# Turning 64x64 adjacency matrices on VectorE instead of TensorE in a four-layer graph network

## The chip, the cores and the metric

The kernel runs on one core of one Trainium2 chip. The metric is the device time of one execution in microseconds (us), taken as the median of several runs; smaller is better. Before the change it is 2506.93 us, the median of three runs between 2506.72 and 2507.49. The profile that this document reads is of one execution with a span of 2505.0 us from its first to its last instruction.

A core has five engines with a queue each. TensorE (PE in the profile, with PEld for its weight loads) multiplies matrices and can turn a 128x128 tile by multiplying with the identity. VectorE (DVE), ScalarE (ACT) and GpSimd (POOL) do elementwise work. SyncE (SP) issues transfers. Each engine takes its own instructions in the order of the program; between engines they wait on semaphores.

## What is computed

The input is 128 graphs of 64 nodes with 256 features each, with one 64x64 adjacency matrix of zeros and ones for each graph. Four layers follow one another, each adding to x what it makes of the normalized x. Cut to what matters:

```python
# layer 0: attention with 8 heads, masked by the adjacency
scores = where(adj > 0, q @ k.T / sqrt(32), -9e15);      x += softmax(scores) @ v @ Wo + bo
# layer 1: attention, biased by the logarithm of the adjacency
scores = q @ k.T / sqrt(32) + log(adj + 1e-6);           x += softmax(scores) @ v @ Wo.T + bo
# layer 2: five rounds of a gated graph network
for l in range(5):
    agg = A.T @ (h @ weight[l])                          # A = (adj != 0)
    h = gru_cell(agg, h)
x += h * mask
# layer 3: gated graph convolution
norm  = (sum(abs(adj), -1) + 1e-6) ** -0.5
f_hom = adj @ (x @ theta * norm) * norm
x += elu(gate * f_hom + (1 - gate) * f_het)
```

Everything is in 32-bit floats.

## The kernel before

Two graphs make a pair and fill 128 partitions; four pairs (512 tokens) make a group, and there are 16 groups. The adjacency of two groups is loaded at once as `adjq`, with the 128 rows of a pair on the partitions and 64 columns for each of 8 pairs in the free dimension.

The adjacency is needed in three forms. The attention works on scores that lie with the keys on the partitions, and multiplies exp(scores) by a mask: for layer 0 `(adj > 0) * 2^32` and for layer 1 `(adj + 1e-6) * 2^32`. Both masks need the adjacency turned. Layer 2 takes it as it lies (`A`). Layer 3 multiplies by its transpose, as a 128x128 matrix for each pair with the two 64x64 blocks on the diagonal, scaled by `norm` (`adjT`).

The kernel is built twice into the program, first in this fast form (`lean`) and then in a careful form that runs only if a test on the data asks for it; on these inputs it does not run.

The masks, at the start of a group's part in the first two layers:

```python
masks = [new(f"mask{layer}", [P, PAIRS, NODES], 2, ...) for layer in range(2)]
ps_m = bank(f"mask_{g}")                                 # one of four PSUM banks
def turn_adj():
    for half in range(2):
        p = first + 2 * half
        nc.tensor.transpose(ps_m[:, half * P : (half + 1) * P],
                            adjq[:, p : p + 2, :].rearrange("p t k -> p (t k)"), ident.tile)
pe(220, turn_adj, [adjq, ident], [ps_m], holds=masks, mode=TURN)
for layer, (by, op) in enumerate(((0.0, ALU.is_gt), (1e-6, ALU.add))):
    vec(dve(256), lambda ...: nc.vector.tensor_scalar(
        masks[layer]..., ps_m[:, : 2 * P], by, MASK_UP, op0=op, op1=ALU.mult), [ps_m], [masks[layer]])
```

And the matrix for layer 3, at the end of that part. `blk` is one tile for the whole kernel, filled with zeros once:

```python
for gp in range(2):
    s = slice(gp * NODES, (gp + 1) * NODES)
    pool(350, lambda s=s: nc.gpsimd.tensor_copy(blk[s, :, s], adjq[s, sel, :]), [adjq], [(blk, gp)])
A = ...                                                  # one VectorE instruction on adjq
...                                                      # deg and norm
ps = bank(f"adjT_{g}")
def turn():
    for p in range(PAIRS):
        nc.tensor.transpose(ps[:, p * P : (p + 1) * P], blk[:, p, :], ident.tile)
pe(437, turn, [blk, ident], [ps], holds=[adjT], mode=TURN)
for p in range(PAIRS):
    sca(act(P, 1), lambda p=p: nc.scalar.activation(
        adjT[:, p, :], ps[:, p * P : (p + 1) * P], AF.Identity, scale=norm[:, p : p + 1]), ...)
```

None of these calls is emitted where it stands. `pe`, `vec`, `vec2`, `sca` and `pool` record an operation with a cost from fixed formulas of the author, and a planner (`Plan.run`) puts all operations of the kernel into the order of each engine. It plays a list scheduling through with those costs, and takes at each step the operation with the lowest key that can start:

```python
def dve(n, ptr=0):                                       # assumed ns of a VectorE operation
    return n * 1.042 + 68 + 60 * ptr
WIDE, T64, T32, TURN = range(4)                          # how TensorE's array is divided
CHANGE = ((0, 95, 95, 0), (250, 30, 135, 200), (237, 135, 30, 187), (0, 95, 95, 0))
BESIDE = 0.45                                            # how much small products are drawn together
...
if mode in (T64, T32):
    return -BESIDE if last in (T64, T32) else ALONE if small < 2 else 0.0
```

So a change of any operation can move every other one. Most products are on the whole 128x128 array (WIDE). Three are on a divided array: the aggregation of layer 2 (`agg`, 64x64, 80 times), the scores (`s`, 64x64, 64 times), and the weighing of the values by the attention (`o`, 32 columns wide, 64 times). `CHANGE` holds what the author takes a change between these to cost.

While one group is in layer 2, the next is in layers 0 and 1 and the one before is in layer 3; the planner interleaves the three.

## Time and profile before

| what | measured |
|---|---|
| time | 2506.93 us |
| TensorE busy | 2483.1 of 2505.0 us |
| VectorE busy | 1875.7 us in 4396 instructions |
| ScalarE busy | 1304.8 us |
| GpSimd busy | 889.4 us |
| turning for the masks | 32 TensorE matmuls |
| turning for layer 3 | 64 TensorE matmuls, after 32 GpSimd copies |
| masks out of PSUM | 32 VectorE instructions, 402 ns each on average |

In the profile a row names a line of the kernel, an engine, an operation, and the tile written and the tiles read; then comes how often it occurs, its busy time in all in us, and the mean duration of one in ns. A product in 32-bit floats shows as two matmul records, since the array takes it in two passes; a transpose shows as one. Matmuls follow one another closer than their durations, because they are pipelined: for what one costs, the distance from its start to the next start is read, and for that the timeline, which lists the instructions of one engine in order of time, with equal neighbours merged. The same holds, less strongly, for VectorE.

### The profile page before, as it was taken

What the parts mean: (1) busy time and instruction counts of PE and PEld (TensorE: products, weight loads), DVE (VectorE), ACT (ScalarE), POOL (GpSimd) and SP (SyncE); (2) the same over time, 40 slices, a digit from 0 to 9 for tenths busy, and PEclk for the clock granted to TensorE, in tenths of its full rate; (3) what the DMA queues carried; (4) which work ended last, traced back from release to release, by engine and by line L of the source; (5) the groups of instructions that cost most, each with busy time, mean ns of one, the idle gap of its engine ahead of it and who ended that gap; (6) DMA issues with size and microseconds to landing.
All of it is one profiled execution on the core that took longest, in us unless ns stands there. A gap on an engine that the chain in (4) does not pass through costs nothing.

```text
span 2505.0 us, 58714 instructions
## 1 busy us (share of the span) xinstructions
PE 2483.1 (99%) x24057; PEld 2131.6 (85%) x24057; DVE 1875.7 (75%) x4396; ACT 1304.8 (52%) x2654; POOL 889.4 (36%) x894
## 2 busy tenths in 40 slices
PE   9999999999999999999999999999999999999997
PEld 7888888888888888888888888888888888888885
DVE  6666777777777777787778777777777777877667
ACT  3455454555555455555554555555554555555544
POOL 6633433333333332423334333333333424333221
PEclk9999999999999999999999999999999999999999
DMA  6411212112222121222113122122221212211120
GB/s 207 171 61 64 94 62 88 65 53 84 72 80 72 62 74 65 82 69 80 59 62 102 50 88 83 52 81 72 80 68 59 76 66 80 72 46 71 49 71 19
DMA packets 78266, 188.60 MB, mean 75 GB/s; under 512 B 14802, under 2 KB 66852, under 8 KB 67108
## 3 DMA queue, kind: packets, MB, share of 16 engines
q1 hardware_dynamic: 77872, 184.71, 21.6%
q8 instruction: 192, 3.15, 0.5%
q14 instruction: 86, 0.70, 0.1%
q10 hardware_dynamic: 116, 0.04, 0.0%
HBM read 166.70 MB, written 18.02 MB: 74 GB/s over the span
## 4 chain that ended last, share of the span: by engine, by line
PE 97%; DVE 2%; ACT 0%; issue 0%; POOL 0%; DMA 0%; DVEq 0%; ACTq 0%; POOLq 0%
PE gb L994 22%; PE gc L994 17%; PE nb L994 11%; PE nc L994 8%; PE qkvb L711 6%; PE qkvc L711 5%; PE y L879 4%; PE agg L1034 3%; PE l3b L1339 3%; PE s L775 2%; PE l3c L1339 2%; PE lnT L547 2%; PE hT L547 2%; PE o L843 2%; PE o L851 1%; PE gv L930 1%
## 5 line engine op out<-in xcount | busy, mean ns | idle before, releaser
L1103 POOL TENSOR_TENSOR sn<-h,sn 128x512 f32<-128x512 f32 x158 | 205.5, 1304 | 664.3 <-ACT sn L1101 664.3
L994 PE MATMUL gb<-Ta,gv 128*128 128x256 f32 x960 | 248.1, 381 | 0.0
L994 PE MATMUL gb<-Th,w_hh 128*128 128x256 f32 x960 | 247.9, 381 | 0.0
L963 POOL TENSOR_TENSOR Th<-h 128x256 f32<-128x256 f32 x160 | 120.4, 772 | 333.6 <-PE nb L994 230.6
L533 POOL TENSOR_TENSOR rstd<-pw,few 128x2 f32<-128x2 f32 x128 | 94.9, 741 | 382.6 <-DVE pw L532 380.6
L799 POOL TENSOR_TENSOR e<-e,mask 128x512 f32<-128x512 f32 x128 | 176.2, 1396 | 105.9 <-ACT e L797 105.9
L994 PEld LDWEIGHTS gb<-Th,w_hh 128*128 128x128 f32 x960 | 177.5, 190 | 23.4 <-issue 1.9
L994 PEld LDWEIGHTS gb<-Ta,gv 128*128 128x128 f32 x960 | 177.1, 191 | 23.4 <-issue 2.1
L1101 ACT ACTIVATE sn<-sn,b_n 128x512 f32<-128x512 f32 x158 | 113.4, 722 | 132.9 <-DVE sn L1099 132.5
L994 PE MATMUL gc<-h,w_hh 128*128 128x256 f32 x640 | 167.4, 384 | 0.1
L994 PE MATMUL gc<-agg,gv 128*128 128x256 f32 x640 | 164.6, 380 | 0.0
L1105 DVE SCALAR_TENSOR_TENSOR sn<-sg,sn 128x512 f32<-128x512 f32 x158 | 107.4, 686 | 62.9 <-POOL sn L1103 62.6
L1086 ACT ACTIVATE sg<-sg,b_rz 128x512 f32<-128x512 f32 x158 | 106.6, 715 | 90.3 <-DVE sg L1066 90.2
L963 POOL TENSOR_TENSOR Th<-h,Th 128x256 f32<-128x256 f32 x160 | 144.8, 905 | 8.6 <-DVE h L1107 2.9
L1097 DVE SCALAR_TENSOR_TENSOR sn<-sg,sn 128x512 f32<-128x512 f32 x158 | 118.6, 758 | 37.1 <-ACT sn L1208 30.5
L994 PE MATMUL nb<-Th,w_hh 128*128 128x256 f32 x480 | 144.5, 383 | 0.1
L994 PE MATMUL nb<-Ta,gv 128*128 128x256 f32 x480 | 144.3, 382 | 0.0
L994 PEld LDWEIGHTS gc<-h,w_hh 128*128 128x128 f32 x640 | 117.0, 190 | 23.4 <-issue 2.5
L879 PE MATMUL y<-w_L_gnn_Wo,oT 128*128 128x256 f32 x512 | 135.6, 380 | 0.1
L994 PEld LDWEIGHTS gc<-agg,gv 128*128 128x128 f32 x640 | 120.7, 190 | 16.0 <-issue 0.2
L1047 DVE TENSOR_TENSOR Ta<-agg 128x256 f32<-128x256 f32 x160 | 88.7, 574 | 50.8 <-PE nb L994 33.0
L1107 DVE SCALAR_TENSOR_TENSOR h<-sn 128x512 f32<-128x512 f32 x158 | 122.2, 780 | 5.6 <-ACT e L797 0.5
(228 smaller groups left out, 6527.2 us busy)
## 6 DMA issues: line engine op xcount, KB each, us to landing
gv<-gates SPq DMA_DIRECT2D x80, 1344.0 KB, 5.9
qw<-kept SPq DMA_DIRECT2D x203, 192.0 KB, 2.5
x<-in_x_dram SPq DMA_DIRECT2D x32, 256.0 KB, 3.4
out_dram<-x SPq DMA_DIRECT2D x32, 256.0 KB, 2.9
gates<-gv SPq DMA_DIRECT2D x5, 1344.0 KB, 4.9
adjq<-in_adj_dram SPq DMA_DIRECT2D x8, 256.0 KB, 5.2
gw<-in_L_gnn_weight_dram SPq DMA_DIRECT2D x5, 256.0 KB, 6.4
kept<-s SPq DMA_DIRECT2D x8, 128.0 KB, 3.4
```

The lines of the kernel that those rows point to most:

```text
L711: nc.tensor.matmul(bk[:, j * P : (j + 1) * P], lhs, rhs, start=first and j == 0, stop=True, skip_group_check=True)
L799: pool(1000, lambda e=e: nc.gpsimd.tensor_tensor(e.tile, e.tile, bias_at(pp)[:, None, :].to_broadcast([P, 4, 2 * NODES]), op=ALU.mult), [e ...
L879: pe(mm(256), lambda i=i, c=c: nc.tensor.matmul(py[:, i * D : (i + 1) * D], oT[:, i, c, :], w_o[:, c, :], start=c == 0, stop=c == 1), [(oT ...
L963: pool(690, lambda: nc.gpsimd.tensor_tensor(T[:, i, :], x(), y(), op=ALU.subtract), reads, [(T, i)])
L994: nc.tensor.matmul(bank_[:, col * HALF : (col + 1) * HALF], at(g, n), rhs(), start=first and j == 0, stop=True, skip_group_check=True)
L1086: sca(act(TOK, 1.5), lambda k=k, col=col: nc.scalar.activation(g_v[:, :, k, :], g_v[:, :, k, :], AF.Tanh, bias=b_rz[:, col : col + 1], sca ...
L1097: vec2(dve(TOK), lambda: nc.vector.scalar_tensor_tensor(a_(), r(), 1.0, a_(), op0=ALU.add, op1=ALU.mult), [*ts[0], n_v], [n_v])
L1101: sca(act(TOK, 1.5), lambda: nc.scalar.activation(a_(), a_(), AF.Tanh, bias=b_n[:, oc : oc + 1]), [n_v, b_n], [n_v])
L1103: pool(1230, lambda: nc.gpsimd.tensor_tensor(b_(), hh(), a_(), op=ALU.subtract), [*hp, n_v], [n_v])
L1105: vec2(dve(TOK), lambda: nc.vector.scalar_tensor_tensor(b_(), z(), 1.0, b_(), op0=ALU.add, op1=ALU.mult), [*ts[1], n_v], [n_v])
L1107: vec2(dve(TOK), lambda: nc.vector.scalar_tensor_tensor(hh(), b_(), 0.5, a_(), op0=ALU.mult, op1=ALU.add), [n_v], hp)
L1339: pe(mm(384), lambda: nc.tensor.matmul(bk[:, : 3 * P], b(), w3[:, :, n, :], start=first, stop=True, skip_group_check=True), [w3, *reads], ...
```

## The change

The turning moves from TensorE to VectorE. VectorE's transpose instruction turns each 32x32 block in place. A 64x64 matrix consists of four such blocks, and a pair of graphs of eight; when the instruction's output starts at another group of 32 partitions than its input, the block is also moved, and with all blocks moved the whole matrix is turned. So neither the identity nor PSUM is needed.

For the masks, 16 instructions for each group take 32 partitions and two pairs' blocks each (32x64 elements), from every one of the four groups of 32 partitions to every one. They write into the tile of layer 1's mask; both masks are then made from that tile, in SBUF, the second in place. For layer 3, 8 instructions (32 partitions, four pairs, 32x128 elements) put the turned blocks directly into `blk`, which takes the place of the two GpSimd copies, the four TensorE transposes and the PSUM bank; ScalarE then scales out of `blk`.

```diff
         if lean:
             masks = [...]
-            ps_m = bank(f"mask_{g}")
-            def turn_adj(): ...            # two nc.tensor.transpose
-            pe(220, turn_adj, [adjq, ident], [ps_m], holds=masks, mode=TURN)
+            adj_part = lambda: adjq[:, sel, :].rearrange("q (half t) k -> q half t k", t=2)
+            turned_adj = lambda: masks[1].tile.rearrange("q (half a) n -> q half (a n)", a=2)
+            for block in range(16):
+                frm, to = block // 4, block % 4
+                vec(dve(64), lambda frm=frm, to=to: nc.vector.transpose(
+                    turned_adj()[to * 32 : (to + 1) * 32, :, frm * 32 : (frm + 1) * 32],
+                    adj_part()[frm * 32 : (frm + 1) * 32, :, to // 2, to % 2 * 32 : (to % 2 + 1) * 32]),
+                    [adjq], [(masks[1], block)])
             for layer, (by, op) in enumerate(((0.0, ALU.is_gt), (1e-6, ALU.add))):
                 vec(dve(256), lambda ...: nc.vector.tensor_scalar(
-                    masks[layer]..., ps_m[:, : 2 * P], by, MASK_UP,
-                    op0=op, op1=ALU.mult), [ps_m], [masks[layer]])
+                    masks[layer].tile, masks[1].tile, by, MASK_UP, op0=op, op1=ALU.mult),
+                    [masks[1]], [masks[layer]])
...
         for gp in range(2):
             s = slice(gp * NODES, (gp + 1) * NODES)
-            pool(350, lambda s=s: nc.gpsimd.tensor_copy(blk[s, :, s], adjq[s, sel, :]), [adjq], [(blk, gp)])
+            if not lean: ...               # as before
+            for block in range(4):
+                frm, to = (slice(lo, lo + 32) for lo in (gp * NODES + block // 2 * 32, gp * NODES + block % 2 * 32))
+                col = slice(block % 2 * 32, (block % 2 + 1) * 32)
+                vec(dve(128), lambda frm=frm, to=to, col=col: nc.vector.transpose(
+                    blk[to, :, frm], adjq[frm, sel, col]), [adjq], [(blk, (gp, block))])
...
-        ps = bank(f"adjT_{g}")
+        ps = blk if lean else bank(f"adjT_{g}")
+        turned_blk = (lambda p: blk[:, p, :]) if lean else (lambda p: ps[:, p * P : (p + 1) * P])
-        pe(437, turn, [blk, ident], [ps], holds=[adjT], mode=TURN)
+        if not lean:
+            pe(437, turn, [blk, ident], [ps], holds=[adjT], mode=TURN)
         for p in range(PAIRS):
             sca(act(P, 1), lambda p=p: nc.scalar.activation(
-                adjT[:, p, :], ps[:, p * P : (p + 1) * P], AF.Identity, scale=norm[:, p : p + 1]),
+                adjT[:, p, :], turned_blk(p), AF.Identity, scale=norm[:, p : p + 1]),
                 [ps, norm], [(adjT, p)])
```

None of the planner's own numbers is changed.

## The prediction

> **What bounds the kernel now.** First the busy times of the page, then its chain that ended last:

> ```profile
> PE 2483.1 (99%) x24057; PEld 2131.6 (85%) x24057; DVE 1875.7 (75%) x4396; ACT 1304.8 (52%) x2654; POOL 889.4 (36%) x894
> ...
> PE 97%; DVE 2%; ACT 0%; issue 0%; POOL 0%; DMA 0%; DVEq 0%; ACTq 0%; POOLq 0%
> ```

> TensorE is busy 99% of the span and makes up 97% of the chain. A table of windows says where the rest lies: from 400 to 2300 us TensorE is busy in 1899.5 of 1900 us; of the 22 us it idles, 17 lie after 2300 us, where the last group has no neighbour to fill in, and most of the others at the start. So there is no wait inside to remove: time is what TensorE's instructions take, one after the other, plus a start and a tail. VectorE, at 75%, has idle time, but it feeds TensorE.

> The rows that the change removes, from the groups of TensorE and GpSimd by shape:

> ```profile
> L1280 PE MATMUL adjT<-ident,adjblk 128*128 128x128 f32 x64 | 9.7, 275 | 0.0
> L1231 PE MATMUL mask<-ident,adjq 128*128 128x128 f32 x32 | 6.2, 274 | 0.0
> L1265 POOL COPY adjblk<-adjq 64x256 f32<-64x256 f32 x32 | 13.1, 411 | 37.4 <-PE adjT L1280 36.4
> ```

> The 275 ns are a duration in a pipeline, not a cost. From the starts in the trace, two transposes in a row are 109 ns apart (median of 981 pairs), and a 128x256 pass 216 ns from the next. GpSimd waits before its copies, but it is idle 64% of the time and bounds nothing.

> The timeline of TensorE shows a second cost, that of dividing the array (start, duration, instruction, count):

> ```profile
> 1166.50 0.38 PE L1231 MATMUL mask<-ident,adjq 128*128 128x128 f32 x2
> 1166.81 0.45 PE L843 MATMUL o<-e,v 64*32 64x64 f32 x32
> ...
> 1214.95 0.59 PE L994 MATMUL nb<-Ta,gv 128*128 128x256 f32 x2
> 1215.48 1.16 PE L1034 MATMUL agg<-A,ht 64*64 64x64 f32 x64
> 1216.57 1.13 PE L994 MATMUL gb<-h,w_hh 128*128 128x256 f32 x4
> ...
> 1185.45 1.03 PE L994 MATMUL gb<-h,w_hh 128*128 128x256 f32 x4
> 1186.41 1.16 PE L1034 MATMUL agg<-A,ht 64*64 64x64 f32 x64
> 1187.39 1.06 PE L775 MATMUL s<-kexp,qk 64*64 64x128 f32 x32
> 1188.38 0.92 PE L994 MATMUL gb<-Ta,gv 128*128 128x256 f32 x3
> ```

> An aggregation alone takes 1216.57 - 1214.95 less two passes of 0.216, that is 1.19 us. Scores alone, read in the same way at 359 us, take 1.13. An aggregation with scores directly behind takes 1188.38 - 1185.45 less four passes: 2.07 instead of 2.32. So a neighbour on the same kind of array saves **0.25 us**. By the same reading a weighing alone takes 1.38 us, and beside an aggregation or scores the pair takes 0.09 less. Before the weighing above stands a transpose, and the array is divided at the same price: the last transpose start to the first `o` start is 203 ns in the trace, 94 more than 109, as it is 309 instead of 216 behind a full product. Taking the transpose away neither saves nor costs a change.

> [...] 294 ns (row L1423, 128x256 out of SBUF) against 402 ns for the masks out of PSUM.

> **The change, part by part.**

> *Removed from TensorE*: 16 groups x (2 + 4) transposes = 96, at 109 ns: **-10.5 us**, all on the path.

> *Moved on TensorE*: the order of the changed program is fixed when it is built, so I counted it. Full-array products and the other transposes are as many as before. The divided ones are not placed as before:

> | what stands together | before | changed |
> |---|---|---|
> | aggregation and scores | 26 | 3 |
> | weighing and scores | 29 | 30 |
> | aggregation and weighing | 14 | 2 |
> | alone (agg, s, o) | 40, 9, 21 | 75, 31, 32 |

> The planner, its weights tuned to the old operations, has lost 23 pairs worth 0.25 us and 11 worth 0.09: 5.8 + 1.0 = **+6.8 us**, on the path. What is left of the gain is 3.7 us.

> *Added to VectorE*: these rows carry the estimate, from the groups of VectorE by shape:

> ```profile
> L863 DVE STREAM_TRANSPOSE zt<-rz 128x256 f32<-128x256 f32 x128 | 50.0, 416 | 0.0
> L732 DVE TENSOR_TENSOR v<-qkvb,q 128x128 f32<-128x128 f32 x58 | 16.4, 282 | 0.0
> L1268 DVE TENSOR_SCALAR A<-adjq 128x256 f32<-128x256 f32 x16 | 15.4, 960 | 11.3 <-PE agg L1034 11.3
> L1236 DVE TENSOR_SCALAR mask<-mask 128x256 f32<-128x256 f32 x32 | 12.5, 402 | 1.7 <-PE mask L1231 1.7
> ```

> A transpose of 256 columns takes 416 ns and an operation of 128 columns 282, so about 1.05 ns a column on 148 ns. Estimate: 148 + 64 x 1.05 = 215 ns for a mask block, 282 for a block of layer 3. If each is held, that is its cost: 256 x 0.215 + 128 x 0.282 = 55 + 36 = 91 us. The 32 mask operations should gain some 0.1 us each, 3.5 us, unless they are slowed as row L1268 is: the same sort of operation, whose 16 instances range from 279 to 1374 ns, the fastest near the 294 of L1423. In the ten slow ones a subtraction on GpSimd (row L1103) had begun 54 to 62 ns earlier, and they end about 150 ns after it: an operation of this sort waits while GpSimd's runs. The planner reckons with this for L1268, but not for the masks, which read PSUM until now. VectorE's busy time becomes about 1963 us, 78% of the span: beside TensorE's work, no bound by its sum.

> *Its bursts*: the planner assumes 64 x 1.042 + 68 = 135 ns for a mask block and 201 for the others. Held, they take 80 ns more each: 1.3 us for the 16 masks of a group, 0.65 us for the 8. In the changed order of a middle group 13 mask blocks stand before and between the subtractions `Ta` of the fifth round, and 5 blocks of layer 3 around those of the first. What follows stands late by these amounts. How much room is there? By TensorE's order, between the end of the aggregation and the first product that reads `Ta` stand 18 us of other products in the fifth round, but only 5.9 in the first; two copies by ScalarE (0.6 each) and the first subtraction (0.42) have to fit in there with their signals, and with the blocks about 1.5 us more. That fits. VectorE's order also holds things with less room, so I allow 0 to 0.4 us of stall a group, **+2 us** with a middle of 0.13 x 16.

> *Removed from GpSimd and PSUM*: 13 us of copies and two of the uses of the four PSUM banks for each group. GpSimd is not the bound, and TensorE has hardly a stall that a free bank could end: 0.

> *The start*: TensorE's first mask turn came at 9.34 us, between projections. Now 16 blocks (about 3.5 us) stand on VectorE before the columns of biases and the first `qk`, which began at 10.44 and 10.70. They come some 1.5 us late; the changed order puts products for the fused weights ahead of the first scores. Within 1 us either way: 0.

> Sum: 2506.9 - 10.5 + 6.8 + 2 = **2505 us**.

> **Rivals.** *Removal counts in full*: if the lost pairs cost less than I read, or the old schedule paid for them elsewhere, 2497 us. Against it: the 0.25 and the 0.09 come from starts in the trace, and the counts from the program. *VectorE's lateness becomes the wait*: if each group stalls TensorE by 1 us, through held blocks and slowed masks, 2519 us. For it speaks that VectorE is in the inner loop (its row `sg` already waits for TensorE's `gc`, and TensorE in turn for it now and then) and that the planner's costs are too low by 2 us a group; against it, that in the before kernel row L1268 overruns its assumed 250 ns by 1.1 us in most groups, and TensorE still runs without a gap. *VectorE as the bound*: 78% is far from it. *A hidden change*, with nothing to measure: 2507, quite possible, for two terms of opposite sign nearly cancel.

> **Range and chances.** The removal is sure to 0.5 us, the pairs to 1.5, the stalls run from 0 to 12, start and tail to 3 either way. So the range is 2497 to 2514. Two per cent are 50 us: TensorE would have to shed five times what is removed, or to stall 3 us in every group. Faster 0.01, within 2% 0.97, slower 0.02.

> **What would show it right or wrong.** TensorE: 96 records fewer, 23961; busy about 2480; no rows for `mask` and `adjT`; aggregation and scores mostly apart in the timeline, still 1.19 and 1.13 us each. VectorE: 384 instructions more, 4780; new transposes near 215 and 282 ns with the next start not before the end; busy near 1963. The mask row: near 294 ns on average if undisturbed, up to 1370 where GpSimd works. If a transpose across quadrants takes 400 ns or more, the bursts double and the stalls with them. If TensorE idles by more than 10 us between 400 and 2300 us, the second rival holds; the waits then name a row of VectorE. If TensorE's busy time falls to 2473, I was wrong on the pairs.

## The result, and the profile after

The changed kernel takes **2575.38 us** (median of four runs, 2573.0 to 2576.19) against 2507.21 for the kernel before beside it: a ratio of **1.027, with an interval of 1.0252 to 1.0288**. It is slower by 68 us. The prediction was 2505 us, and its range ended at 2514.

The page of the changed kernel, first the busy times, then the chain that ended last:

```profile
PE 2509.7 (98%) x23961; PEld 2132.1 (83%) x23961; DVE 1962.5 (76%) x4780; ACT 1306.0 (51%) x2654; POOL 865.3 (34%) x862
...
PE 79%; DVE 15%; ACT 3%; issue 2%; POOL 0%; DMA 0%; DVEq 0%; ACTq 0%
```

TensorE has its 96 records fewer, and yet is busy 27 us longer. VectorE's share of the chain rose from 2% to 15%. The span is 2572.9 us, of which TensorE now idles 63 instead of 22. So two questions: what is TensorE waiting for, and why does less work take it longer?

The list of waits answers the first (us in all, times, longest). First the row of the kernel before, then of the changed one:

```profile
PE gc L994 <- DVE sg L1066: 0.6, 2, 0.4
```

```profile
PE gc L994 <- DVE sg L1066: 28.2, 24, 2.1
```

`gc` is a PSUM bank with gate sums of layer 2, and `sg` is VectorE's addition that reads it. The next products into the bank wait until it is read, up to 2.1 us by the row above:

```python
vec(dve(512), lambda: nc.vector.tensor_tensor(dst_at(), src(), other.tile, op=ALU.add), [bk, other], writes)   # sg, L1066
```

The timeline shows one such place, first TensorE (start, duration, instruction, count, idle time before it and its releaser):

```profile
925.58 0.59 PE L879 MATMUL y<-w_L_gnn_Wo,oT 128*128 128x256 f32 x2
926.01 0.60 PE L547 MATMUL lnT<-ident,xn 128*128 128x128 f32 x4
928.72 2.05 PE L994 MATMUL gc<-Th,w_hh 128*128 128x256 f32 x4 [2.11 <-DVE sg L1066]
930.56 1.76 PE L994 MATMUL gc<-Ta,gv 128*128 128x256 f32 x4
932.16 0.60 PE L994 MATMUL nc<-Th,w_hh 128*128 128x256 f32 x2
```

and VectorE in the same stretch:

```profile
921.47 2.22 DVE L1230 STREAM_TRANSPOSE mask<-adjq 32x64 f32<-32x64 f32 x9
923.72 0.43 DVE L1047 TENSOR_TENSOR Ta<-agg 128x256 f32<-128x256 f32 x1
924.18 0.98 DVE L1230 STREAM_TRANSPOSE mask<-adjq 32x64 f32<-32x64 f32 x4
...
926.30 0.74 DVE L1230 STREAM_TRANSPOSE mask<-adjq 32x64 f32<-32x64 f32 x3
927.08 0.69 DVE L1097 SCALAR_TENSOR_TENSOR sn<-sg,sn 128x512 f32<-128x512 f32 x1
927.69 0.29 DVE L1235 TENSOR_SCALAR mask<-mask 128x256 f32<-128x256 f32 x1
927.89 0.68 DVE L1066 TENSOR_TENSOR sg<-gc,p1g 128x512 f32<-128x512 f32 x1
```

VectorE has no gap: 16 mask blocks, four `Ta`, one `sn`, one mask, and only then `sg`, which ends at 928.57. TensorE's last product before it ends at 926.61, and it goes on at 928.72. From the last use of `gc` (the four passes just before 925.15) to its next stand only two passes for `nc`, two for `y` and one turn `lnT` of four transposes: 1.3 us of work, and VectorE is late by more. In this way 11 of the groups each lose 2.27 us, the distance from the last transpose to the next pass, 2.38, less the usual 0.109.

The second question is answered by what follows the wait. The four passes at 928.72 take until 930.56, 1.84 us; in the kernel before four take 4 x 0.216 = 0.86. The table of windows shows why (window, us, busy time and count of PE, PEld, DVE, ACT, POOL, then TensorE's clock, the share of DMA and its GB/s):

```profile
921.00:926.00 5.00, 5.00 (x24) 4.34 (x24) 4.74 (x18) 1.52 (x3) 3.85 (x6) 1.00 0.65 230
926.00:929.00 3.00, 0.89 (x6) 0.67 (x5) 2.93 (x8) 0.60 (x1) 0.00 (x0) 0.94 0.21 81
929.00:932.50 3.50, 3.50 (x10) 2.83 (x10) 3.50 (x11) 0.86 (x2) 1.27 (x1) 0.56 0.00 0
932.50:936.00 3.50, 3.50 (x21) 3.17 (x20) 2.03 (x7) 2.03 (x5) 1.71 (x2) 1.00 0.01 2
```

After the idle time of 2.11 us the granted clock is 0.5 for 3.41 us (the trace's record of the clock; the window's 0.56 is its mean over 3.5 us), and 10 instructions stand where the next window has 21. This costs another 1.7 us, half of the 3.41. It happened after 9 of the 11 waits and once at the start, after an idle time of 3.0 us: 10 x 1.7 = 17 us. This is most of why TensorE's busy time grew with less to do: in experiment 3, which has none of these drops, it is 2492.4 us.

The new instructions, from the tile views of the changed kernel (count: duration in ns, least, median and most, first and last start in us):

```profile
L1230 DVE STREAM_TRANSPOSE mask<-adjq x256: 199/236/242, 8.2 to 2025.5; 32x64 f32<-32x64 f32 x128
...
L1235 DVE TENSOR_SCALAR mask<-mask x32: 281/294/984, 12.5 to 2030.1; 128x256 f32<-128x256 f32 x32
```

```profile
L1270 DVE STREAM_TRANSPOSE adjblk<-adjq x128: 265/302/309, 45.8 to 2070.2; 32x128 f32<-32x128 f32 x128
```

From one mask block's start to the next are 250 ns (median of 211 pairs with nothing between), against 236 ns of duration; for layer 3 it is 315 against 302. So each starts 13 to 14 ns after the end of the one before (this is what "held" means here and in the recorded texts), while the `Ta` at 925.19 and 925.53 above start 0.34 us apart and last 0.43. The planner, which assumed 135 and 201, is 115 ns short for each.

### The profile page after: what moved, and what is told of

Read it like the earlier page. It is cut to its first block, busy times and chain, and to the rows that moved or that the text cites. A ratio compares the mean times of both kernels' runs of the same rounds, so it can differ in the third digit from the quotient of the medians.

```text
span 2572.9 us, 58794 instructions
## 1 busy us (share of the span) xinstructions
PE 2509.7 (98%) x23961; PEld 2132.1 (83%) x23961; DVE 1962.5 (76%) x4780; ACT 1306.0 (51%) x2654; POOL 865.3 (34%) x862
## 4 chain that ended last, share of the span: by engine, by line
PE 79%; DVE 15%; ACT 3%; issue 2%; POOL 0%; DMA 0%; DVEq 0%; ACTq 0%
PE gb L994 19%; PE gc L994 14%; PE nb L994 9%; PE nc L994 6%; PE qkvb L711 5%; PE qkvc L711 4%; PE y L879 3%; PE agg L1034 3%; PE l3b L1347 2%; DVE mask L1230 2%; DVE Ta L1047 2%; PE o L843 2%; PE s L775 2%; PE l3c L1347 2%; PE hT L547 2%
## 5 line engine op out<-in xcount | busy, mean ns | idle before, releaser
L1103 POOL TENSOR_TENSOR sn<-h,sn 128x512 f32<-128x512 f32 x158 | 205.0, 1301 | 802.7 <-ACT sn L1101 802.7
L994 PE MATMUL gb<-Th,w_hh 128*128 128x256 f32 x960 | 250.9, 384 | 0.0
L994 PE MATMUL gb<-Ta,gv 128*128 128x256 f32 x960 | 246.5, 379 | 0.0
L799 POOL TENSOR_TENSOR e<-e,mask 128x512 f32<-128x512 f32 x128 | 182.9, 1449 | 69.5 <-ACT e L797 68.6
L994 PEld LDWEIGHTS gb<-Th,w_hh 128*128 128x128 f32 x960 | 177.9, 192 | 30.4 <-DVE sg L1066 4.0
L994 PEld LDWEIGHTS gb<-Ta,gv 128*128 128x128 f32 x960 | 179.3, 190 | 23.1
L1105 DVE SCALAR_TENSOR_TENSOR sn<-sg,sn 128x512 f32<-128x512 f32 x158 | 122.2, 774 | 76.1 <-POOL sn L1103 75.8
L994 PE MATMUL gc<-h,w_hh 128*128 128x256 f32 x640 | 166.1, 382 | 0.1
L994 PE MATMUL gc<-agg,gv 128*128 128x256 f32 x640 | 164.3, 379 | 0.0
L994 PE MATMUL nb<-Ta,gv 128*128 128x256 f32 x480 | 144.4, 382 | 0.0
L994 PE MATMUL nb<-Th,w_hh 128*128 128x256 f32 x480 | 143.1, 380 | 0.0
L963 POOL TENSOR_TENSOR Th<-h,Th 128x256 f32<-128x256 f32 x160 | 133.4, 834 | 9.3 <-DVE h L1107 2.7
L1107 DVE SCALAR_TENSOR_TENSOR h<-sn 128x512 f32<-128x512 f32 x158 | 131.7, 840 | 5.7 <-DVE sn L1105 0.5
L994 PEld LDWEIGHTS gc<-h,w_hh 128*128 128x128 f32 x640 | 117.7, 190 | 21.4 <-ACT sg L1093 0.5
L1097 DVE SCALAR_TENSOR_TENSOR sn<-sg,sn 128x512 f32<-128x512 f32 x158 | 118.2, 756 | 20.1 <-ACT sn L1208 12.5
L1093 ACT ACTIVATE sg<-sg,b_rz 128x256 f32<-128x256 f32 x158 | 71.6, 500 | 121.8 <-DVE sg L1066 119.8
L994 PEld LDWEIGHTS gc<-agg,gv 128*128 128x128 f32 x640 | 118.6, 190 | 17.3
```

What stands on the lines that cost most here:

```text
L799: pool(1000, lambda e=e: nc.gpsimd.tensor_tensor(e.tile, e.tile, bias_at(pp)[:, None, :].to_broadcast([P, 4, 2 * NODES]), op=ALU.mult), [e ...
L963: pool(690, lambda: nc.gpsimd.tensor_tensor(T[:, i, :], x(), y(), op=ALU.subtract), reads, [(T, i)])
L994: nc.tensor.matmul(bank_[:, col * HALF : (col + 1) * HALF], at(g, n), rhs(), start=first and j == 0, stop=True, skip_group_check=True)
L1097: vec2(dve(TOK), lambda: nc.vector.scalar_tensor_tensor(a_(), r(), 1.0, a_(), op0=ALU.add, op1=ALU.mult), [*ts[0], n_v], [n_v])
L1103: pool(1230, lambda: nc.gpsimd.tensor_tensor(b_(), hh(), a_(), op=ALU.subtract), [*hp, n_v], [n_v])
L1105: vec2(dve(TOK), lambda: nc.vector.scalar_tensor_tensor(b_(), z(), 1.0, b_(), op0=ALU.add, op1=ALU.mult), [*ts[1], n_v], [n_v])
```

## The experiments

The theories at the beginning, in short: the held transposes make `sg` late (by their length, by their burst, or through a planner that reckons them too short); the order of the program, which moved with the change, is worse by itself; the change for layer 3 matters as much as the one for the masks. Ratios are always to the kernel before, run beside.

**1. The same order without the transposes.** The instructions of each engine stay in the order of the changed kernel, but the 256 mask transposes are left out; the masks are then made of the unturned adjacency.

```diff
-                vec(dve(64), lambda frm=frm, to=to: nc.vector.transpose(...),
+                vec(dve(64), lambda: None,
...
-                    masks[layer].tile, masks[1].tile, by, MASK_UP, op0=op, op1=ALU.mult),
+                    masks[layer].tile, adjq[:, sel, :], by, MASK_UP, op0=op, op1=ALU.mult),
```

> The 256 transposes for the masks are left out; the masks are made from the adjacency as it lies, so they belong to other graphs. The order of all other instructions is that of the changed kernel. Theory (the burst of mask transposes makes VectorE late, TensorE waits 2.26 us for a PSUM bank in 11 groups, and its clock is then halved for 3.4 us, 1.7 us lost each time): about 44 us of the 68 go, 2524 to 2534, and the clock stays at 1.0 after the start. Rival (the new order as such, with its lost pairs and its start, is what costs): 2560 or more.

Measured: 2528.04 us, 1.008 (1.0063 to 1.0097). The 256 transposes account for 47 of the 68 us. No stall of 2 us is left, and between 400 and 2300 us the mean clock is 1.00 as before.

The same with those of layer 3 left out too (its matrix is then zero):

```diff
-                vec(dve(128), lambda frm=frm, to=to, col=col: nc.vector.transpose(
-                    blk[to, :, frm], adjq[frm, sel, col]), [adjq], [(blk, (gp, block))])
+                vec(dve(128), lambda: None, [adjq], [(blk, (gp, block))])
```

> All 384 new transposes are left out, for the masks and for layer 3 (whose matrix then stays zero); the order of all other instructions is that of the changed kernel. If the prediction's sum for TensorE (10.5 us off, 6.8 us on for lost pairs) was right and all else comes from the transposes: 2500 to 2508. Rival (the new order costs more than the pairs, in its start and in small stalls, whatever VectorE does): 2512 to 2530.

Measured: 2517.21 us, 1.0038 (1.0024 to 1.0052). Layer 3's transposes cost 10.8 us in this order. Without any transpose it is still 8.3 us slower than before, though TensorE has 10.5 us of transposes less. In the starts of the trace, the distances inside the divided blocks are together 7.3 us longer than before; those between passes on the full array exceed their usual ones by 3.4 us more than before, and those at a change between the two kinds by 3.6. These are many small waits, no repeated large one. So the second theory holds for a smaller part: this order is worse even when the transposes are free. And the third holds by a fifth of what the transposes cost: 11 us for layer 3, 47 for the masks.

**2. One half of the change alone.** First layer 3 by VectorE and the masks by TensorE as before, then the reverse. Each is an order of its own.

```diff
-            for block in range(16): ...                              # masks, VectorE
+            pe(220, turn_adj, [adjq, ident], [ps_m], holds=masks, mode=TURN)
```

> Half of the change: masks turned by TensorE as before, layer 3 by VectorE. Its pairs by the program: 16 us-level terms are 3.5 us worse than before, 7.0 us of transposes removed. Theory (mask bursts are the cost): 2503 to 2513. Rival (any held transposes on VectorE stall TensorE, in proportion to their time, 37 of 97 us): about 2530.

Measured: 2526.67 us, 1.0074 (1.0057 to 1.0091). No stall of 2 us, but 14 us above the range of the theory and near the rival's 2530.

```diff
-            if not lean:                                             # layer 3's copies and turns
+            if True:
```

> The other half: masks by VectorE, layer 3 turned by GpSimd and TensorE as before. Pairs 6.7 us worse, 3.5 us of transposes removed. Theory (mask bursts are the cost): 2550 to 2572, with clock drops after stalls of 2 us. Rival (in proportion to the time of the held transposes): about 2545, without drops of the clock; or, if the half of layer 3 is the guilty one, 2510.

Measured: 2583.39 us, 1.03 (1.0283 to 1.0317): the masks alone are as bad as the whole change, and 11 us worse than the theory's range. The rival that the loss is in proportion to the held time (2545) fails too. The two halves lose 18 and 75 us, more together than the whole with its 68: each is an order of its own, so the halves cannot be added, and which share the masks have is read from experiment 1. The same row of waits has 24.3 us in 11 times, and at 10 places two products of layer 3 are another 1.1 us apart; the rest was not traced. Here the clock fell behind idle times of 2.2 to 2.5 us only 2 times in 11 (the mean clock of the profiled run is 0.996, of the changed kernel's 0.992). So the drop of the clock isn't sure after a wait of this length, and the stalls hurt without it.

**3. Is it that they are held?** The transposes write to the partitions that they read from, so that most stay in the same group of 32 partitions (a quadrant, in the expectation below) as the one before. Their number and size are unchanged, but each matrix is turned only within its blocks of 32x32, which stay on their partitions.

```diff
-                    turned_adj()[to * 32 : (to + 1) * 32, :, frm * 32 : (frm + 1) * 32],
+                    turned_adj()[frm * 32 : (frm + 1) * 32, :, to * 32 : (to + 1) * 32],
...
-                    blk[to, :, frm], adjq[frm, sel, col]), ...
+                    blk[frm, :, to], adjq[frm, sel, col]), ...
```

> As many transposes of the same size in the same order, but each writes into the 32 partitions that it reads, so that the quadrant changes every fourth (masks) or second time (layer 3) instead of every time; blocks stay in the wrong quadrant, so the masks and layer 3's matrix hold other entries. Theory (a transpose that changes the quadrant is held until the one before has ended, 250 ns instead of 135 from start to start, and that lateness makes the stall): starts 135 ns apart within a quadrant, the stall of 2.26 us shrinks by over 1 us, no drops of the clock: 2530 to 2545. Rival (number and place of the instructions count, not the hold): 2570 or more, starts still about 250 ns apart.

Measured: 2543.73 us, 1.0143 (1.0126 to 1.016), 32 us less than the change. The timeline of this kernel, first VectorE, then TensorE:

```profile
905.47 1.49 DVE L1230 STREAM_TRANSPOSE mask<-adjq 32x64 f32<-32x64 f32 x9
906.99 0.78 DVE L1047 TENSOR_TENSOR Ta<-agg 128x256 f32<-128x256 f32 x1
907.80 0.74 DVE L1230 STREAM_TRANSPOSE mask<-adjq 32x64 f32<-32x64 f32 x4
908.58 0.74 DVE L1047 TENSOR_TENSOR Ta<-agg,Ta 128x256 f32<-128x256 f32 x1
```

```profile
910.02 0.60 PE L547 MATMUL lnT<-ident,xn 128*128 128x128 f32 x4
912.17 1.10 PE L994 MATMUL gc<-Th,w_hh 128*128 128x256 f32 x4 [1.56 <-DVE sg L1066]
913.11 1.03 PE L994 MATMUL gc<-Ta,gv 128*128 128x256 f32 x4
```

Nine blocks take 1.49 us where they took 2.22. Of the 211 distances from start to start, 100 are 120 to 140 ns, 64 are 160 to 180, and 46, where the quadrant changes, 200 to 220; the mean is 158 instead of about 250. That moving a block is slow in itself is ruled out by the trace of the changed kernel: the four blocks of a group that stay on their partitions stand 244 to 254 ns from their neighbours, like the others (one distance, with another wait in it, left out). So the length goes with the change of quadrant: 250 ns where the output's quadrant changes each time, 120 to 180 where it stays. The stall went from 2.27 to 1.72 us, less than the 1.2 us by which the blocks ahead of `sg` became shorter. The other 0.66 is lost on the two `Ta` in the lines above, which took 0.43 each in the changed kernel: they now begin while a subtraction of GpSimd (`Th`) runs, and in all 11 groups both end 0.28 us after it. (The changed kernel has such places too: of its 64 `Ta` that begin while a `Th` runs, 50 end 0.28 us after it and take 0.50 to 0.98 us.) With 1.56 us of idle time the clock did not fall behind any of the 11 waits: the four passes at 912.17 take 0.94 us, and from 400 to 2300 us the mean clock is 1.00. So of the 32 us, 11 x 0.55 = 6 come from these waits, some 17 from the clock (the drop at the start is gone too), 4 from a second wait for `sg` that is 0.38 us shorter in 10 groups, and most of the rest from the first 150 us.

**4. Give TensorE something to do.** Work is added: one turn in each of 12 groups, the one ahead of the wait, is done five times over, 16 transposes more.

```diff
+        again = 5 if tag[0] == "lnT" and tag[2:] == ["0", "0"] and int(tag[1]) >= 4 else 1
...
+                for _ in range(again):
                     nc.tensor.transpose(to, src_at(i), ident.tile)
```

> The changed kernel with work added: in groups 4 to 15 the four transposes that TensorE runs just before the stall are run five times each, 16 more of 109 ns = 1.74 us, with the same results. Theory (the stall is long enough to have the clock halved for 3.4 us, which costs 1.7 us each time): TensorE is busy in most of the wait, the clock stays at 1.0, and the kernel becomes faster by 11 x 1.7 = 19 us: 2555 to 2560. Rival (the drops of the clock cost nothing, as TensorE would wait for others then anyhow): 2573 to 2580.

Measured: 2558.94 us, 1.0204 (1.0187 to 1.0221): **16 us faster than the change with 192 matmuls more**, which by 109 ns are 21 us of work. The timeline of TensorE (lines are shifted by three in this kernel):

```profile
920.02 2.35 PE L550 MATMUL lnT<-ident,xn 128*128 128x128 f32 x20
922.74 1.10 PE L997 MATMUL gc<-Th,w_hh 128*128 128x256 f32 x4 [0.37 <-DVE sg L1069]
923.67 1.03 PE L997 MATMUL gc<-Ta,gv 128*128 128x256 f32 x4
```

The wait is nearly filled, the passes behind it run at full pace, and the core's mean clock is 0.998 instead of 0.992. Work put into the gap costs little, as TensorE would have idled; what is won is the clock, which now drops at the start only: nine drops fewer, by 1.7 us 15 of the 16. So the drops are a consequence of the idle time, and their 17 us a cost of their own.

**5. Tell the planner the truth.** The measured 250 and 315 ns take the place of the assumed ones.

```diff
-                vec(dve(64), ...          # masks: 135 ns
+                vec(250, ...
-                vec(dve(128), ...         # layer 3: 201 ns
+                vec(315, ...
```

> The changed kernel, with the planner told what the new transposes cost when held: 250 and 315 ns instead of 135 and 201. Theory A (the planner's ignorance is what hurts; VectorE has 24% idle time): the stall behind the mask burst vanishes, 2505 to 2520. Theory B (VectorE has no room for the bursts between the operations that TensorE waits for, whoever orders them): other waits take its place, 2530 to 2560.

Measured: 2543.71 us, 1.0142 (1.0125 to 1.0159). Half of the loss is gone, but the wait has moved, as the list of waits of this kernel shows:

```profile
PE l3b L1347 <- DVE hTT L1336: 12.2, 10, 1.3
PE l3b L1347 <- ACT hT L552: 7.5, 11, 0.7
```

Products of layer 3 now wait for operands that VectorE and ScalarE prepare. With the transposes also made less urgent than anything else that could start:

```diff
-                               key=lambda t: t[1].key + self.shift(mode, t[1].mode, small))
+                               key=lambda t: t[1].key + t[1].lazy + self.shift(mode, t[1].mode, small))
...
-                    [adjq], [(masks[1], block)])
+                    [adjq], [(masks[1], block)], lazy=0.1)      # the same for layer 3
```

> As true_costs, and the new transposes come last among the operations that VectorE could start (a tenth of a group's length added to their key in the choice). Theory A: like true_costs or up to 5 us better. Theory B: 2525 to 2555; if it lies more than 10 us below true_costs, the urgency of the masks was part of the cost.

Measured: 2543.19 us, 1.0142 (1.0126 to 1.0159): no different. Yielding at a choice was not what was missing.

**6. Plan anew.** `FRONT` and `STEP` are numbers of the planner that place the next group's attention and the rounds of layer 2 against each other; the author's values stand with the old operations. Three orders with the true costs and other numbers, picked from many by their pairs and by the room behind VectorE's blocks, and as a control the kernel before with its `FRONT` moved by 0.01:

```diff
-FRONT = 0.1
+FRONT = 0.13                              # and the true costs of experiment 5
```

> true_costs with one more number changed: FRONT, the point at which a group's first two layers begin in the plan, 0.13 instead of 0.1, so that the planner finds another order (pairs by the program: 13 aggregations beside scores, 13 beside weighings, 19 of weighings and scores). All work on VectorE stays, held transposes included. Theory C (what was lost is the order that had been tuned to the old operations; another order has room for the transposes): 2495 to 2512, no stall of over 1 us that comes back in each group. Theory B (VectorE has no room, in any order): 2525 or more.

Measured: 2510.54 us, 1.0011 (1.0004 to 1.0018). The timeline of VectorE shows a group's 16 blocks in pieces:

```profile
763.38 0.73 DVE L1230 STREAM_TRANSPOSE mask<-adjq 32x64 f32<-32x64 f32 x3
764.43 0.48 DVE L1230 STREAM_TRANSPOSE mask<-adjq 32x64 f32<-32x64 f32 x2
765.40 0.74 DVE L1230 STREAM_TRANSPOSE mask<-adjq 32x64 f32<-32x64 f32 x3
773.97 1.99 DVE L1230 STREAM_TRANSPOSE mask<-adjq 32x64 f32<-32x64 f32 x8
```

and in its list of waits, the row of `gc` for `sg` is gone but for one:

```profile
PE gc L994 <- DVE sg L1066: 0.4, 1, 0.4
```

```diff
+FRONT = 0.07                              # and the true costs
```

> As tuned_013 with FRONT = 0.07 (14 aggregations beside scores, 12 beside weighings, 18 of weighings and scores). Theory C: 2495 to 2512. Theory B: 2525 or more.

Measured: 2511.36 us, 1.0012 (1.0006 to 1.0019).

```diff
+FRONT = 0.07                              # and the true costs
+STEP = -0.03
```

> As tuned_007 with STEP = -0.03 as well, which starts the rounds of layer 2 earlier in the plan (16 aggregations beside scores, 15 beside weighings, 30 of weighings and scores: 1.9 us better than the other two in divided products). Theory C: 2493 to 2510. Theory B: 2525 or more.

Measured: 2525.32 us, 1.0066 (1.005 to 1.0083), a miss. By its number of pairs this order should have been faster than the last one; but at 11 places products wait for the addition `v` (L732), 1.13 us each, which the counts don't show.

```diff
-FRONT = 0.1
+FRONT = 0.09                              # in the kernel before
```

> The kernel before, without the change, with FRONT = 0.09 instead of 0.1: a control of how much a bare move of the order costs. Pairs by the program are 26 of aggregation and scores, 9 and 9 of the others, about 2.3 us worse than before. Theory C (the order before had been tuned to a sharp optimum, so nearly any disturbance loses some 20 us): 2515 to 2535. Rival (the order is robust, and only the transposes on VectorE upset it): 2507 to 2512.

Measured: 2538.09 us, 1.0122 (1.0105 to 1.0139). **The kernel before loses 31 us when that one number moves from 0.1 to 0.09.** Lost pairs account for 2 of them by the count; for the rest no single wait stands out. So it stands on an optimum that is narrow at least on this side, and a new order easily lies beside it.

**7. What is left.** First the best order so far with the transposes left out as in experiment 1, to see what they cost where they fit:

> tuned_013 with all 384 transposes left out (masks from the adjacency as it lies, layer 3's matrix zero), the order of everything else the same. If the held transposes still cost something in this order: 2500 to 2505, 5 to 10 us below tuned_013. If the order hides them: 2508 to 2511, as tuned_013; the missing 6 us are then small stalls of the order itself.

Measured: 2502.84 us, 0.998 (0.9972 to 0.9988). So the transposes cost about 8 us (2510.5 - 2502.8) even here (how much of it is the hold was not measured), and without them this order is 5.4 us faster than the kernel before (2508.27 beside it). By the prediction's terms it should be: -10.5 for the transposes and, by its pairs, +4.2, that is -6.3.

```diff
-FRONT = 0.1
-STEP = 0.0
+FRONT = 0.14                              # and the true costs
+STEP = -0.02
```

> true_costs with FRONT = 0.14 and STEP = -0.02: by the program 24 aggregations beside scores, 26 beside weighings, 18 of weighings and scores; 10.1 us less than before for transposes and divided products together. Theory C (the order decides): 2497 to 2507 if it has no more stalls than before. Theory B' (held transposes cost a rest of some 8 us in any order): 2506 to 2515.

Measured: 2507.56 us, 1.0 (0.9992 to 1.0008). This order has nearly the pairs of the kernel before again: aggregations alone 30 times, with scores 24 and with weighings 26 times. By the durations of the prediction that is within 0.4 us of the kernel before on divided arrays, so TensorE has 10 us less to do, and the time is the same to 2 us. It is the best that was found for VectorE's transposes: as fast as before, not faster.

```diff
+FRONT = 0.125                             # and the true costs
```

> true_costs with FRONT = 0.125: 15 aggregations beside scores, 14 beside weighings, 18 of weighings and scores; 6.7 us less than before for transposes and divided products together. Theory C: 2500 to 2510, near tuned_013. Theory B': 2508 to 2516.

Measured: 2515.72 us, 1.0033 (1.0021 to 1.0045). It is a neighbour of 0.13 in number and in pairs, and 5 us slower: two rows of small waits of 0.2 to 0.3 us, 12 times each. It misses the range of the theory that the order alone decides (2500 to 2510); this run and the one before fit a cost of some 8 us that the transposes keep in these orders too.

## Why the prediction was wrong, point by point

The sum that the runs give, in place of 2506.9 - 10.5 + 6.8 + 2: the removal and the lost pairs, -3.7; small waits of the new order itself, +12 (by subtraction: the 8.3 of the second run of experiment 1, less -3.7); layer 3's transposes, +11; the masks' transposes, +47, which are 11 waits of 2.27 us (25), 10 drops of the clock (17), and 5 of other waits, mostly at the start. Together +66 of the 68 us; the rest lies within what the times of the kernel before, run beside the experiments, differ by (2507.2 to 2508.9).

- **The removal** held: 96 records fewer. That it is worth 10.5 us was not measured alone; in the first run of experiment 7 it came out together with the pairs, at 5.4 for 6.3 expected.
- **The pairs** held: an aggregation alone and scores alone keep their distances in the changed kernel, 1.19 us (median of 17) and 1.13 (of 13), and so do the pairs: an aggregation with scores 2.06 (of 2; before 2.06, of 22), a weighing with scores 2.41 (of 29; before 2.42, of 27). Of the 20 us that the second run of experiment 1 lost against the removal, in the profiled spans (2514.6 - 2505.0 + 10.5), 14 are found as small waits (7.3 + 3.4 + 3.6), which leaves 6 beside the 6.8.
- **VectorE's load** held: 1962.5 us busy (1963 predicted), 4780 instructions, 294 ns for the undisturbed mask operation. But the sum came out by luck. The blocks were sized too small, 250 instead of 215 ns and 315 instead of 282 from start to start; their durations add up to 98.8 us and not 91. The mask operations gained nothing (13.9 us in all, 12.5 before, where 3.5 less were predicted), since some were slowed, up to 984 ns. And other rows became shorter, `A` alone by 10 us, which no term foresaw. That the transposes would be held was an assumption of the prediction, which the trace of before does not show; the changed kernel's trace (250 ns from start to start at 236 of duration) and experiment 3 show it: mostly 120 to 140 ns within a quadrant, against 250 when it changes each time.
- **The step that failed is the +2 us for the bursts.** The prediction checked the room for `Ta` alone, 18 and 5.9 us, then wrote that "VectorE's order also holds things with less room" and allowed 0 to 0.4 us a group without looking for it. The operation with the least room was `sg`, named under the rivals as one that TensorE waits for "now and then": 1.3 us between two uses of the bank that it reads. The view to look at was VectorE's order behind the burst, operation by operation, with the TensorE instruction that each of them releases. Measured: 2.27 us in 11 groups, 25 us in place of the 2, and 17 more by the clock.
- **The rival "VectorE's lateness becomes the wait" was right in kind** and sized at 1 us a group, 12 us over the base; the masks came to 47. The argument against it, that row L1268 overruns by 1.1 us in most groups without a gap, was about another place in the order, with other room.
- **The clock was in no term.** A wait was taken to cost its length; here 2.27 us became 3.97 in 9 cases of 11, 1.6 times its length on average. The clock record of the changed kernel shows where the drops lie. The clock is first full at 7.03 us; each of the ten drops until TensorE's last product lasts 3.41 us and begins a whole multiple of 3.413 us after that (29 to 592 times). Cut TensorE's time up to that product at these multiples: the stretch just ahead of a drop was idle for 59 to 62%, the one at the start for 89%, and no other stretch for more than 41%. Nine of the waits of 2.1 us fall into one stretch each; the other two are split over two (26 and 36%, 41 and 21%) and cost no clock. The 1.56 us of experiment 3 fill at most 46% of a stretch. In the kernel before, cut in the same way, no stretch is idle for more than 35%, and the clock stays full from 7.08 us until after TensorE's last product. What the clock does between 46 and 59% these figures do not show. That so many hit in the changed kernel looks like a coincidence of lengths: half of its waits follow the one before after 157.0 to 157.1 us, and 46 stretches are 157.0.
- **"None of the planner's own numbers is changed"** was taken as a source of lost pairs alone. The control of experiment 6 shows that an order beside the tuned one can cost 31 us by itself, so the range of the prediction, 17 us wide, was too narrow for a change that moves the plan.

Still open: TensorE has four waits ahead of weighings (`o`) in the order without transposes, 2.5 us in all, for which the profile names no releaser and which the kernel before hardly has. And whether an order exists that keeps some of the 10 us; none of those tried did.

## What to carry to other kernels

When work moves to an engine with idle time, its mean load says nothing about the wait: write down, for everything that stands behind the new burst in that engine's order, which instruction of the bounding engine it releases and how much work that engine has in hand until then. Where a planner or scheduler orders the program, give it measured costs of the new operations and tune it again before judging the change, and treat a small move of its numbers in the old kernel as a control. And a wait of TensorE can cost more than its length: in the changed kernel 2.27 us became 3.97, 1.75 times its length, at the 9 of 11 places where the granted clock then was 0.5 for 3.41 us, and stayed 2.27 at the other two.
